# Layer 0's layernorm taken into the loop over heads, its row factors made before the dense sums, and layer 1's constants loaded in layer 0

## The chip, the cores and the metric

The kernel runs on one core of a Trainium2 chip. The metric is the device time of one execution in microseconds (us). Each version was run several times, always beside runs of the kernel before on the same chip. Every run that is compared here is in the fast state. Single executions scatter more than one would like: the kernel before took 4556 to 4594 us over all its runs. The adjacency product of the last layer alone took between 250 and 269 us from trace to trace. So causes are read from the lengths of stages in the traces, which for the stages in question repeat within 1 us, and the total is used only to check them.

## The reference

Four layers follow each other, each as `x = layernorm(x + layer(x))`, over 4096 nodes of 256 features with a 0/1 adjacency. The first two matter here:

```python
# layer 0: eight heads of 32 columns
feats  = (x @ W.T + b).reshape(n, 8, 32)
logit  = leaky_relu(parent[:, None, :] + child[None, :, :], 0.2)   # n x n x heads
logit  = where(adj != 0, logit, 0.0)
out0   = einsum('ijh,jhc->ihc', softmax(logit, axis=1), feats)
# layer 1
out1   = (diagonal(adj) + adj) @ (x @ weight) + bias
```

## The kernel before

The exponential of a leaky sum factors: for one row the terms with a positive sum are a row factor times a column factor, and the others a second such product. So layer 0 needs, for each head, a sum over the neighbours whose sum is positive (a mask that depends on the head) and sums over all neighbours and all nodes (which do not). The latter are the dense sums. Layer 0 is therefore: a prelude (features, logits), the dense sums, the loop over heads, and a closing.

```python
for half in range(2):                      # four heads each
    for it in range(4):                    # a pass: 1024 rows = 8 blocks
        # SyncE: na = packed adjacency of the pass; gm = factored features of the half
        for hh in range(4):                # a head
            # GpSimd's queue: lpb = this head's row logits for 1024 rows, z = its dense sums
            for g in range(8):             # 512 neighbours
                gt = work.tile([P, K, IT], FP8, name="gt", bufs=4)   # masks
                sg = work.tile([P, K, IT], FP8, name="sg", bufs=3)   # signs
                if g % 8 in (2, 5, 7):     # VectorE: 4 comparisons, 1 "and"
                    ...
                else:                      # ScalarE: 4 signs; VectorE: shift and "and"
                    ...
                # TensorE: 32 matmuls with gt as weights
            # VectorE: epilogue of the head (reduce, 6 operations on row factors, divide)
        nc.gpsimd.dma_start(yd[...], y)    # to DRAM
# closing, after the loop: 16 times
nc.sync.dma_start(xs, xr[:, b:b + 2, :]); nc.scalar.dma_start(y, self.yd[b:b + 2]...)
nc.vector.tensor_add(xs, xs, y)
self.layernorm(work, xs, xs)               # statistics on VectorE, power on GpSimd, normalisation on VectorE
```

Layer 1 then loads its weight, bias and the diagonal of the adjacency, makes the support `x @ weight` for 32 blocks, and multiplies it by the adjacency, whose pieces (`adj_piece`) come on SyncE's queue through five buffers. In each of the 32 blocks GpSimd adds one row to X, VectorE adds the product, and a layernorm follows. The order of instructions on each engine is chosen by a scheduler from a timing model, and memory is handed out by pools: a pool that is opened where a closed one lay waits for the closed one's last users (two such waits below took 9.69 and 15.0 us).

## Time and profile before

| | kernel before |
|---|---|
| time | 4570.63 us, median of 3 runs |
| dense sums, first to last matmul | 73.7 to 632.4 us |
| loop over heads | 647.4 to 1352.5 us |
| layer 1's first transpose | 1412.8 us |
| layer 1's last support matmul | 1468.6 us |
| layer 1's adjacency product from there | 246.2 us |

Read such a table by its seams. TensorE is the busiest engine (93% of the span), so the time in which it stands still between two stages is what a reordering may win. The prediction shows the lines.

### The profile page before, as it was taken

The page shows a single profiled execution, that of the slowest core. Times are in us where ns is not written, and L with a number is a line of the kernel's source. Part 1 is how long each engine was busy: PE and PEld are TensorE (multiplying, and loading weights), DVE is VectorE, ACT ScalarE, POOL GpSimd, SP SyncE. Part 2 cuts the span into 40 slices and gives each one's busy share as a digit, 9 for nine tenths or more (in the row PEclk, how much of TensorE's full clock was granted, in tenths as well). Part 3 has the DMA queues.
Part 4 walks back from the last instruction along what each step waited for, and adds up shares of the span by engine and source line. Part 5 has one row for each costly group of instructions (what it writes and reads, how often), then busy time and mean ns, then how long its engine had stood idle before and what let it go on. Part 6 is the DMA issues. An engine that isn't in the chain of part 4 may idle for free. (4 is left out here: it accounts for less than half of the span.)

```text
span 4576.5 us, 71037 instructions
## 1 busy us (share of the span) xinstructions
PE 4252.9 (93%) x25625; PEld 3414.1 (75%) x25625; DVE 3241.1 (71%) x7512; ACT 2638.7 (58%) x5404; POOL 458.8 (10%) x798
## 2 busy tenths in 40 slices
PE   8889989999985999999999999887899999999898
PEld 6889989999984786677777777665666666666676
DVE  6432249999983225977777777488989999999233
ACT  5443359999961005766666666257677777775100
POOL 1344420000002210000000000001000000000010
PEclk9899999999997999999999999999999999999999
DMA  5889972342323884112222222540122222222697
GB/s 164 295 305 318 313 278 79 113 145 78 107 85 90 288 293 148 39 61 79 80 92 86 79 79 78 193 125 30 39 77 74 78 78 78 78 78 77 215 319 256
DMA packets 314075, 637.08 MB, mean 139 GB/s; under 512 B 42855, under 2 KB 114279, under 8 KB 313703
## 3 DMA queue, kind: packets, MB, share of 16 engines
q1 hardware_dynamic: 193734, 421.22, 28.6%
q0 software_dynamic: 34944, 113.54, 7.0%
q10 hardware_dynamic: 85024, 97.58, 6.3%
q8 instruction: 207, 3.39, 0.3%
q14 instruction: 166, 1.35, 0.1%
HBM read 470.71 MB, written 161.48 MB: 138 GB/s over the span
## 5 line engine op out<-in xcount | busy, mean ns | idle before, releaser
L1174 PE MATMUL ps_a<-X,aT 128*128 128x256 f32 x4096 | 963.8, 387 | 26.9 <-ACT aT L1171 26.7
L1174 PEld LDWEIGHTS ps_a<-X,aT 128*128 128x128 f32 x4096 | 762.6, 191 | 292.3 <-ACT aT L1171 135.7
L275 PE MATMUL acc<-gm,gt 128*128 128x198 bf16 x8192 | 701.4, 248 | 14.3 <-DVE sg L260 10.4
L275 PEld LDWEIGHTS <-gt 128*128 128x128 fp8e4 x8192 | 698.7, 97 | 16.9 <-DVE sg L260 10.5
L267 ACT ACTIVATE sg<-lpb,nlc 128x1024 fp8e4<-128x1024 f32 x640 | 670.9, 1135 | 36.4 <-DVE gt L269 19.3
L427 PE MATMUL pz<-src,ar 128*128 128x264 f32 x4096 | 519.4, 289 | 40.1 <-DVE ar L416 39.5
L427 PEld LDWEIGHTS pz<-src,ar 128*128 128x128 f32 x4096 | 513.4, 192 | 46.2 <-DVE ar L416 44.3
L154 PE MATMUL ps_r<-XD,adj_piece 128*128 128x512 f32 x2048 | 508.5, 400 | 14.5 <-DMA adj_piece<-adjs 14.3
L1171 ACT COPY aT<-ps_tp 128x512 f32<-128x512 f32 x512 | 277.4, 583 | 358.6 <-PE ps_tp L1169 354.4
L909 ACT ACTIVATE ja<-e,nc 128x2048 uint8<-128x2048 f32 x240 | 478.7, 1995 | 0.5 <-issue 0.2
L154 PEld LDWEIGHTS ps_r<-XD,adj_piece 128*128 128x128 f32 x2048 | 382.6, 190 | 113.8 <-DMA adj_piece<-adjs 28.0
L836 PE MATMUL ps_logit<-kT,q 64*128 64x512 f32 x1024 | 462.4, 637 | 4.0 <-ACT e L840 3.8
L855 DVE SCALAR_TENSOR_TENSOR v<-e,c 128x4096 bf16<-128x4096 f32 x100 | 447.2, 4472 | 7.3 <-ACT c L883 6.5
L991 DVE MAX8 cand<-v 128x8 f32<-128x256 f32 x1024 | 360.5, 411 | 2.2
L82 POOL TENSOR_SCALAR ln_var<-ln_mv 128x1 f32<-128x1 f32 (+1 forms) x144 | 52.0, 361 | 2972.0 <-DVE ln_mv L80 2733.4
L1038 DVE SCALAR_TENSOR_TENSOR e<-e,edge 128x512 f32<-128x512 f32 x512 | 347.4, 747 | 1.5
L419 ACT ACTIVATE nb<-a 128x512 uint8<-128x512 f32 x256 | 159.4, 630 | 308.2 <-DMA a<-in_adjt_dram 278.0
L1169 PE MATMUL ps_tp<-ident,e 128*128 128x128 f32 x2048 | 273.3, 275 | 38.7 <-DVE e L1038 25.8
L987 DVE SCALAR_TENSOR_TENSOR v<-e,hi 128x2048 f32<-128x2048 f32 x128 | 300.9, 2351 | 1.7
L1169 PEld LDWEIGHTS ps_tp<-ident,e 128*128 128x128 f32 x2048 | 241.9, 142 | 77.2 <-DVE e L1038 29.3
L840 ACT ACTIVATE e<-ps_logit 128x1024 f32<-128x1024 f32 x256 | 261.2, 1021 | 49.7 <-PE ps_logit L836 28.9
L260 DVE TENSOR_SCALAR sg<-lpb,nlc 128x1024 fp8e4<-128x1024 f32 x384 | 273.5, 750 | 2.1
(298 smaller groups left out, 5085.1 us busy)
## 6 DMA issues: line engine op xcount, KB each, us to landing
adj_piece<-adjs SPq DMA_DIRECT2D x256, 512.0 KB, 6.1
adj_piece<-adjs SPq DMA_DIRECT2D x512, 256.0 KB, 3.5
a<-in_adjt_dram SPq DMA_DIRECT2D x256, 256.0 KB, 4.9
adjs<-ar POOLq DMA_DIRECT2D x256, 256.0 KB, 5.5
na<-nad SPq DMA_DIRECT2D x64, 512.0 KB, 4.4
nad<-nb POOLq DMA_DIRECT2D x128, 128.0 KB, 4.7
lpb<-lpd POOLq DMA_DIRECT2D x32, 512.0 KB, 4.2
xfd<-part ACTq DMA_DIRECT2D x63, 256.0 KB, 2.0
```

The lines of the kernel that those rows point to most:

```text
L154: nc.tensor.matmul(ps, a[:, k, :], rhs(jc).rearrange("p s d -> p (s d)"), start=(jc == 0 and own is None), stop=(jc == self.NB - 1))
L267: nc.scalar.activation(sg[:, k, :], lpb, AF.Sign, scale=-1.0, bias=nlc[:, jc, h:h + 1], saturate=False)
L275: nc.tensor.matmul(acc[:, q, :6 * C1], gt[:, k, q * P:(q + 1) * P], gm[:, jc, hh, :], start=(jc == 0 and q % 2 == 0), stop=(jc == NB - 1 a ...
L427: nc.tensor.matmul(pz[q][:, t, :W], ar[:, q, k, :], src[:, jc, t, s], start=(jc == 0 and s == 0), stop=(jc == NB - 1 and s == 1))
L836: nc.tensor.matmul(pl[:, s, :], q[s * A:(s + 1) * A, :], kT[s * A:(s + 1) * A, c * 512:(c + 1) * 512], start=True, stop=True)
L855: nc.vector.scalar_tensor_tensor(junk, e, c, e, op0=ALU.is_ge, op1=ALU.mult, accum_out=S)
L909: nc.scalar.activation(ja, e[:, s * HALF:(s + 1) * HALF], f, bias=nc1, accum_out=fs[:, i + s:i + s + 1])
L987: nc.vector.scalar_tensor_tensor(v, ec, hi, ec, op0=ALU.is_lt, op1=ALU.mult, accum_out=sb[:, s:s + 1])
L991: nc.vector.max(cand[:, 8 * j:8 * j + 8], v[:, k * 256:(k + 1) * 256])
L1038: nc.vector.scalar_tensor_tensor(ec, ec, edge[:, j:j + 1], ec, op0=ALU.is_ge, op1=ALU.mult)
L1169: nc.tensor.transpose(pt[:, k * P:(k + 1) * P], e[:, jc * P:(jc + 1) * P], self.ident)
L1174: nc.tensor.matmul(pa[:, :D], aT[:, k * P:(k + 1) * P], X[:, jc, :], start=(jc == 0), stop=(jc == NB - 1))
```

## The change

The intent: fill the pauses around the heads' loop. The row factors move ahead of the dense sums, so the seam between dense sums and heads gets shorter and the dense results can be stored already multiplied; the residual and the layernorm of a pass are done when its second half is ready, within the loop; layer 1's weight, bias and diagonal are loaded early. The core of the diff, with cuts:

```diff
     def open_x(self):
-        pool = ...tile_pool(name="x", bufs=1)
+        pool = ...tile_pool(name="x", bufs=1, side="right")
...
-            self.sums0(both, lpd, nad, zd, gmd)
-            (row factors fac from lp, lc: 3 reductions, transpose, maximum, exponentials)
-            nc.sync.dma_start(self.fits, fits)
+            self.sums0(both, nlc, fac, lpd, nad, zd, gmd)   # makes fac and fits before its loop
+            self.open_x()
+            self.load1()                                    # w1, bias1: pool on the right, ScalarE's queue
...
+                    if half:
+                        nc.sync.dma_start(X[:, i0:i0 + Q, :], xr[:, i0:i0 + Q, :])
+                        y0 = work.tile([P, Q, D // 2], F32, name="y0", bufs=1)
+                        nc.sync.dma_start(y0, yd[i0:i0 + Q].rearrange("b p d -> p b d"))
...
-                        (six operations on fac and z)
+                        nc.vector.tensor_mul(red, red, fac[:, 0:2, ...])   # one multiply for both factors
+                        nc.vector.tensor_add(t1, t1, red[:, :, 1, :])
+                        nc.vector.tensor_add(t1, t1, z)
...
+                    for q in range(0, Q, 2):
+                        xs = X[:, i0 + q:i0 + q + 2, :]
+                        nc.vector.tensor_add(xs[:, :, :D // 2], xs[:, :, :D // 2], y0[:, q:q + 2])
+                        nc.vector.tensor_add(xs[:, :, D // 2:], xs[:, :, D // 2:], y[:, q:q + 2])
+                        self.layernorm(work, xs, xs)
...
-    def close0(self): (the closing loop)
...
-            w1 = self.load_w(...); bias = ...; diag = ... (layer 1's loads)
```

## The prediction

> **What bounds the kernel now.** I read the page first (one core, TensorE busy 93% of the 4576.5 us span), then the groups of instructions in layer 0, the busy time by stretches, and last the timeline around the three seams that the change touches. By the starts of the groups, layer 0 runs as: a prelude up to 73.7 us, the dense sums to 632.6, the heads' loop from 647.4 to 1352.7, the closing of layer 0 to 1409.4; layer 1's adjacency product starts at 1476.5. Layers 2 and 3 follow and keep their code. From the groups of the first 2000 us:
>
> ```profile
> L275 PE MATMUL acc<-gm,gt 128*128 128x198 bf16 x8192 | 701.4, 248 | 14.3 <-DVE sg L260 10.4 <-DVE gt L262 2.0 <-DVE gt L269 1.4
> L267 ACT ACTIVATE sg<-lpb,nlc 128x1024 fp8e4<-128x1024 f32 x640 | 670.9, 1135 | 36.4 <-DVE gt L269 19.3 <-DVE gt L262 11.9 <-DMA lpb<-lpd 5.1
> L427 PE MATMUL pz<-src,ar 128*128 128x264 f32 x4096 | 519.4, 289 | 40.1 <-DVE ar L416 39.5 <-ACT total L382 0.5
> ```
>
> TensorE waits only 14.3 us in the whole heads' loop, 10.4 of it before the first matmul, and 40.1 us in the dense sums. The busy time by stretches says how near the other engines are (columns: TensorE, its weight loads, VectorE, ScalarE, GpSimd, then clock, DMA share, GB/s):
>
> ```profile
> 900.00:1000.00 100.00, 100.00 (x1178) 100.00 (x1176) 99.17 (x136) 97.25 (x93) 8.15 (x11) 1.00 0.40 127
> 1100.00:1200.00 100.00, 100.00 (x1178) 100.00 (x1176) 99.18 (x135) 96.27 (x93) 9.60 (x12) 1.00 0.32 94
> ```
>
> 1178 matmuls in 100 us are 0.085 us each, and 256 of them 21.75 us per head. But VectorE is 99% and ScalarE 97% busy: three engines are level, and work added to VectorE here is not free. The seams, from the timeline:
>
> ```profile
> 633.16 0.43 DVE L434 TENSOR_TENSOR zt<-total,pz 128x264 f32<-128x264 f32 x1 [1.33 <-ACT zt L433]
> 638.25 1.15 ACT L267 ACTIVATE sg<-lpb,nlc 128x1024 fp8e4<-128x1024 f32 x1 [5.12 <-DMA lpb<-lpd]
> 641.75 0.34 SPq L239 DMA_DIRECT2D na<-nad  x1
> 647.40 10.72 PE L275 MATMUL acc<-gm,gt 128*128 128x198 bf16 x96 [10.37 <-DVE sg L260]
> ...
> 1352.77 1.81 DVE L280 TENSOR_REDUCE red<-acc 128x528 f32<-128x1584 f32 x1 [5.97 <-PE acc L275]
> 1408.69 0.74 DVE L90 TENSOR_SCALAR X<-X,ln_mv,ln_rstd 128x256 f32<-128x256 f32 x2 [1.13 <-POOL ln_rstd L83]
> 1412.81 1.94 PE L102 MATMUL ps_tp<-ident,X 128*128 128x128 f32 x8 [60.08 <-DVEq L452]
> 1418.54 3.75 PE L639 MATMUL ps_sup<-w,xT 128*128 128x256 f32 x8 [3.06 <-DMA w<-in_w_dram]
> 1429.85 0.18 DVE L632 CAST dg<-diag 128x32 fp32r<-128x32 f32 x1 [16.28 <-DMA diag<-in_adjt_dram]
> 1430.44 3.75 PE L639 MATMUL ps_sup<-w,xT 128*128 128x256 f32 x8 [7.93 <-DVE XD L121]
> ```
>
> TensorE stands still 14.8 us between dense sums and heads (the mask loads behind the row factors start only at 641.75), 60 us for the last head's epilogue, the residual with layernorm and the branch, and again until 1430.44 for layer 1's weight and for the diagonal, behind which VectorE, in order, holds the split of the support.
>
> [...] the closing is a regime of its own, with no matmul for 60 us, but the regime it is moved into has VectorE at 99%. [...] The trace has 430 ns as duration and, by successive starts in a head's epilogue (1336.19, 1336.53, 1336.87), 340 ns as pitch. [...] The diagonal is 4096 elements; its load was issued at 1413.79 and was waited for until 1429.85. [...] The first eight matmuls of layer 1 take 3.75 us, later eights 1.99; that price stays.
>
> **The change part by part.**
>
> *Closing.* Removed from the path: the loop over 16 pairs of blocks between 1360.0 and 1409.4, 49.4 us or 3.1 us a pair, of which VectorE works about 2.4 and otherwise waits for GpSimd's power. Only the last pass's four pairs still follow the last matmul: 4 x 3.1 = 12.4 us. The last head's epilogue shrinks from 5.1 us (1352.77 to 1357.8) to about 4.2 (one multiply of 528 elements, 0.71, and two additions of 0.46 in place of six operations, each waiting for the one before). Then the branch, 3.4 us as now. From last matmul to end of layer 0: 56.7 before, 4.2 + 12.4 = 16.6 after. **-40 us.**
>
> *Layer 1's start.* Weight and diagonal lie ready. The second eight matmuls need only the first eight's split: transposes and copies to about 2.3 us after the branch, matmuls cold 3.75, so about 5.5 us after the branch in place of 17.6. **-12 us.**
>
> *Dense to heads.* The loads of mask and factored rows were behind the transfer of the fits flag; in the changed order the first waits for the last matmul and an adjacency write, so near 634 instead of 641.75. Then the row `lpb` limits, as before at 638.2; four signs at 1.04 and one shift-and-mask of 1.22 let matmuls start near 644 instead of 647.4. The first head took 27.75 us by its starts, 6 over the rule, since mask and factored rows (1.3 MB a group) came at 3.3 us a group; most of that goes too. Layer 1's weight load stands ahead of the signs in ScalarE's queue and takes some back. **-7 us**, and another -1 for small waits in the early heads.
>
> *Heads, VectorE.* The epilogue has three multiplies and adds fewer net: 6 x 0.34 = 2.06 become 0.62 + 2 x 0.34 = 1.30, so a head needs 20.7 in place of 21.5 us (12 comparisons at 0.67, 8 masks at 1.15, the reduction 1.72, the rest), against TensorE's 21.75. In the first half this buys nothing. In the second half each pass of four heads gets 8 additions (0.34), 8 statistics (0.33), 8 aggregations (0.08) and 8 normalisations (0.33), 8.6 us, and in the built order they stand nearly in one piece, so that GpSimd's answers are waited for: with 2.6 us of such waits and 1.1 of dependences, 12.3 us, like the 12.4 of the closing. A pass can spare 4 x 1.05 = 4.2 us: a lack of 8.1. Three passes have this inside the loop. For the first I stepped through the order: six groups of masks are ready, TensorE has work to 16.3 us after the head's start, the next group comes at 17.7 and the one after at 22.8, a stall of 3.7. After that no lead is left, and each of the other two costs near 8. Sum 19, and I take 18 as ScalarE and VectorE may fill some waits. **+18 us.**
>
> *Prelude.* The factors now stand before the dense sums, which share the PSUM banks of their transposes: three reductions, transpose, maximum, matmul and copy delay the first dense matmul from 73.7 to about 77: +3.2. The diagonal's load now meets the first loads, where the transfers are saturated from 4 to 12 us; 3479 of its packets ran in the four microseconds from 1424, so it is some 5 us of transfer time beside others: +0.8. **+4 us.**
>
> *Dense sums.* VectorE gets three more operations per block (32 x 3 x 0.43 = 41 us) but waits 225 us there; ScalarE loses 11.8. From 316 us on TensorE never lacks data and the added work, about 2 us at a pair's seam, fits in the 3.9 us that a piece takes. In the first five pairs, where VectorE and ScalarE hold one another up and TensorE loses 9 us a pair, it may cost up to 2 each. **+3 us.**
>
> Sum: 4570.6 - 40 - 12 - 7 - 1 + 18 + 4 + 3 = 4535.6.
>
> **Rivals.** (a) The layernorm is free in the heads' loop: TensorE is the bound there and VectorE's epilogue got shorter. For it: TensorE's wait is 14.3 us. Against: VectorE's 99%. It would give 4518. (b) VectorE becomes the bound of the whole second half, ScalarE's signs (20.8 us of 21.75 a head, through three buffers) lose their rhythm after every burst, and the stall is 35 us or more: 4553. Against: after a burst each head gains 1 us. (c) The dense sums pay: the longer chain before a result's store, and a GpSimd and ScalarE queue that waits in order, repeats the early stalls; 10 to 15 us more: 4548. For it: those stalls are of just this kind; against: the later pairs have 0 to 0.7 us of stall. (d) The waits at layer 1's start are only exchanged for another, say the adjacency pieces: 4545. Against: five pieces are loaded ahead and the support takes over 35 us.
>
> **Range and chances.** The terms are uncertain by about 8 (heads), 7 (dense), 4 (seam), 4 (layer 1) and 4 (closing), together some 13; a range of 1.6 times that either side: 4514 to 4556. Two per cent would be 91 us, more than all that the removed waits hold together (60 + 14.8 + 17.6); slower by as much would need stalls five times those worked out. So within 2% is nearly sure.
>
> **What would show it.** Right: TensorE's gap before layer 1's transposes about 20 us, not 60; the second eight matmuls of the support 5 to 6 us after the branch; VectorE near 100% after the second half's first pass, with three clusters of TensorE waits on masks, 4, 8 and 8 us, each early in a pass; the first half at 21.75 us a head. Wrong: heads of the second half without stalls (rival a), stalls in every head (b), a dense stage longer than 565 us (c), or any change of over 3 us in layers 2 and 3, whose order of instructions I compared and found the same.

## The result, and the profile after

The changed kernel took 4562.97 us (median of 4 runs) against 4571.07 us for the kernel before in the same rounds; the ratio is 0.9975, with a 95% interval of 0.9956 to 0.9995. Ratios here are the mean time of one kernel's fast runs over that of the other's of the same rounds, so not quite the ratio of the two medians. In a second set with 12 runs the ratio was 0.9968. So the change wins 8 to 15 us where 35 were foreseen; 4535.6 was predicted, and the result lies 7 us above the range (4514 to 4556). That it would stay within 2% came true.

The stages of both profiled runs, from the starts of matmuls (us):

| stage | before | after | difference | foreseen |
|---|---|---|---|---|
| first dense matmul at | 73.7 | 76.4 | +2.7 | +4 |
| dense sums | 558.7 | 552.7 | -6.0 | +3 |
| last dense matmul to first heads' matmul | 15.0 | 18.6 | +3.6 | -3 |
| heads 1 and 2 | 50.5 | 46.9 | -3.6 | -4 |
| heads 3 to 32 | 654.6 | 682.5 | +27.9 | +17 |
| last heads' matmul to layer 1's transposes | 60.3 | 19.4 | -40.9 | -40 |
| from there to the last support matmul | 55.8 | 41.6 | -14.2 | -12 |
| layer 1's adjacency product | 246.2 | 253.8 | +7.6 | 0 |

The table ends with layer 1. From there to the end the two traces took 2861.8 and 2869.0 us, a second trace of the changed kernel 2856.0, and two traces of one other kernel (a_early and c_early2) 2872.9 and 2857.8. So the +7.2 of this pair is scatter, and the prediction's sign "any change of over 3 us in layers 2 and 3" cannot be read from single traces.

The groups of instructions of the changed kernel that answer to the three that the prediction shows (same columns; the lines have other numbers in this kernel):

```profile
L242 PE MATMUL acc<-gm,gt 128*128 128x198 bf16 x8192 | 710.2, 250 | 37.7 <-issue 18.3
...
L234 ACT ACTIVATE sg<-lpb,nlc 128x1024 fp8e4<-128x1024 f32 x640 | 670.5, 1135 | 76.5 <-DVE gt L236 38.3
L450 PE MATMUL pz<-src,ar 128*128 128x264 f32 x4096 | 520.9, 290 | 32.5 <-DVE ar L439 26.0
```

TensorE's wait grew from 14.3 to 37.7 us and ScalarE's from 36.4 to 76.5. Part of this stands ahead of the first matmul, in the seam (10.4 us of TensorE's wait before, 18.3 after). Within the loop TensorE's wait grew from 3.9 to 19.4 us, and nearly all of it ends with a mask (`gt`) that VectorE makes. That is the first place to look. The busy time in the 30 us around the end of the second half's first pass, in the kernel before and then in the changed one (columns as in the prediction's second fence):

```profile
1086.00:1116.00 30.00, 30.00 (x355) 30.00 (x354) 29.77 (x40) 28.64 (x29) 2.72 (x4) 1.00 0.29 92
```

```profile
1086.00:1116.00 30.00, 25.14 (x275) 24.28 (x273) 26.38 (x52) 21.34 (x21) 6.58 (x10) 0.94 0.13 42
```

Where TensorE did 355 matmuls, it now does 275. The timeline of the changed kernel says what happens in it (start, length, engine, line, operation, count, and the idle time before with what ended it):

```profile
1099.80 0.75 DVE L267 TENSOR_TENSOR X<-X,y 128x256 f32<-128x256 f32 x2
...
1102.86 0.73 DVE L91 TENSOR_SCALAR X<-X,ln_mv,ln_rstd 128x256 f32<-128x256 f32 x2 [0.86 <-POOL ln_rstd L84]
...
1106.78 1.19 DVE L236 SCALAR_TENSOR_TENSOR gt<-sg,na 128x1024 uint32<-128x1024 uint32 x1
...
1108.00 4.27 ACT L234 ACTIVATE sg<-lpb,nlc 128x1024 fp8e4<-128x1024 f32 x4 [5.27 <-DVE gt L236]
...
1108.02 4.55 PE L242 MATMUL acc<-gm,gt 128*128 128x198 bf16 x32 [2.88 <-DVE gt L236]
...
1114.54 5.66 PE L242 MATMUL acc<-gm,gt 128*128 128x198 bf16 x45 [1.97 <-DVE gt L229]
```

From 1099.80 to 1106.78 VectorE does nothing but layernorm: a clump, as the layernorm of a whole pass in nearly one piece is called below. ScalarE has filled its three buffers of signs and stands for 5.27 us, TensorE runs out of masks for 2.88 us, and the 32 matmuls after that take 4.55 us instead of 2.72: the array's clock has fallen (0.94 over these 30 us, 1.00 before). The next masks come at 1114.54, after another wait of 1.97 us. Heads 21, 25 and 29, the first of each pass with such a clump, took 29.98, 31.44 and 29.82 us; nearly all others took 21.76.

The seam between dense sums and heads, in the changed kernel:

```profile
629.46 2.28 ACTq L463 DMA_DIRECT2D zd<-zt  x2
630.33 0.33 SPq L202 DMA_DIRECT2D na<-nad  x1
630.80 0.54 POOL L213 DMA_DIRECT2D lpb<-lpd  x1 [7.08 <-DVE deg L459]
...
641.05 0.41 ACTq L110 DMA_DIRECT2D w<-in_w_dram  x1
641.07 0.18 DVE L636 CAST dg<-diag 128x32 fp32r<-128x32 f32 x1 [9.69 <-DMA zd<-zt]
...
642.16 10.50 ACT L234 ACTIVATE sg<-lpb,nlc 128x1024 fp8e4<-128x1024 f32 x10 [20.96 <-DVE sg L227]
```

The loads of masks do start early, at 630.33 instead of 641.75. But layer 1's tiles lie on memory that the last dense results (`zt`) used, so the weight's load and the diagonal's conversion wait until those results are stored, which takes until 641, over 9 us after their issue where such a store took 4.8 us in the median before. That the masks' loads, which now stand beside those stores, slow them is likely; no run changed that alone. The signs stand behind the weight's load in ScalarE's queue.

The start of layer 1, where the kernel before had waits of 60.08, 3.06 and 7.93 us:

```profile
1396.49 1.94 PE L103 MATMUL ps_tp<-ident,X 128*128 128x128 f32 x8 [19.10 <-DVEq L272]
1398.30 3.78 PE L645 MATMUL ps_sup<-w,xT 128*128 128x256 f32 x8
...
1402.09 2.12 PE L645 MATMUL ps_sup<-w,xT 128*128 128x256 f32 x8
```

That part is as foreseen. Its adjacency product is not; first TensorE's timeline there in the kernel before, then in the changed one:

```profile
1476.54 20.15 PE L154 MATMUL ps_adj<-XD,adj_piece 128*128 128x512 f32 x88
1501.81 11.18 PE L154 MATMUL ps_adj<-XD,adj_piece 128*128 128x512 f32 x40 [5.12 <-issue]
```

```profile
1446.02 17.18 PE L155 MATMUL ps_adj<-XD,adj_piece 128*128 128x512 f32 x75
1474.71 14.91 PE L155 MATMUL ps_adj<-XD,adj_piece 128*128 128x512 f32 x56 [11.51 <-DMA adj_piece<-adjs]
```

TensorE waits 11.51 us for a piece. The waits of SyncE's queue in the changed kernel from 1390 to 1480 us (total, times, longest) hold this line:

```profile
SPq L152 <- POOL ln_var L83: 15.0, 1, 15.0
```

A load waited 15 us for GpSimd. In the built order (the one that the scheduler made) it is the 11th: a 256 KB piece that is fetched ahead for layer 2, and layer 1's own pieces, of 512 KB, stand behind it. In the kernel before, five such 256 KB pieces were issued from 1418.3 to 1430.2, while layer 1 still made its support, and held up nothing; here the first was issued at 1469.4. So the order of this queue did change.

### The profile page after: what moved, and what is told of

It is laid out like the page before. It is cut to its first block, busy times and chain, and to the rows that moved or that the text cites. A ratio compares the mean times of both kernels' runs of the same rounds, so it can differ in the third digit from the quotient of the medians.

```text
span 4560.9 us, 70953 instructions
## 1 busy us (share of the span) xinstructions
PE 4263.9 (93%) x25625; PEld 3423.7 (75%) x25625; DVE 3254.6 (71%) x7529; ACT 2630.8 (58%) x5373; POOL 458.0 (10%) x794
## 3 DMA queue, kind: packets, MB, share of 16 engines
q1 hardware_dynamic: 197700, 423.31, 28.3%
## 5 line engine op out<-in xcount | busy, mean ns | idle before, releaser
L1180 PE MATMUL ps_a<-X,aT 128*128 128x256 f32 x4096 | 964.2, 387 | 28.9 <-ACT aT L1177 28.8
L242 PE MATMUL acc<-gm,gt 128*128 128x198 bf16 x8192 | 710.2, 250 | 37.7 <-issue 18.3
L234 ACT ACTIVATE sg<-lpb,nlc 128x1024 fp8e4<-128x1024 f32 x640 | 670.5, 1135 | 76.5 <-DVE gt L236 38.3
L155 PEld LDWEIGHTS ps_r<-XD,adj_piece 128*128 128x128 f32 x2048 | 382.7, 189 | 114.0 <-DMA adj_piece<-adjs 27.9
```

Source lines behind the costliest of these rows:

```text
L155: nc.tensor.matmul(ps, a[:, k, :], rhs(jc).rearrange("p s d -> p (s d)"), start=(jc == 0 and own is None), stop=(jc == self.NB - 1))
L234: nc.scalar.activation(sg[:, k, :], lpb, AF.Sign, scale=-1.0, bias=nlc[:, jc, h:h + 1], saturate=False)
L242: nc.tensor.matmul(acc[:, q, :6 * C1], gt[:, k, q * P:(q + 1) * P], gm[:, jc, hh, :], start=(jc == 0 and q % 2 == 0), stop=(jc == NB - 1 a ...
L1180: nc.tensor.matmul(pa[:, :D], aT[:, k * P:(k + 1) * P], X[:, jc, :], start=(jc == 0), stop=(jc == NB - 1))
```

## The experiments

All results were correct. "Heads stage" is from the first to the last heads' matmul: 705.1 us before, 729.4 and 728.8 in two traces of the changed kernel. The last columns of the table are the stretches that the change was about, all from the profiled runs:

| run | ratio to before | gap + heads 1, 2 | heads stage | to transposes | to last support | adjacency |
|---|---|---|---|---|---|---|
| before | 1 | 65.5 | 705.1 | 60.3 | 55.8 | 246.2 |
| changed (a_again) | 0.9968 | 65.4 | 728.8 | 19.4 | 41.4 | 254.4 |
| a_row | 0.9955 | 65.4 | 729.1 | 19.2 | 41.6 | 249.6 |
| a_late | 0.9971 | 64.2 | 730.5 | 19.2 | 40.4 | 254.5 |
| a_early | 0.9984 | 65.2 | 705.0 | 59.1 | 40.8 | 255.9 |
| c_early2 | 0.9993 | 65.9 | 705.1 | 59.6 | 41.3 | 255.9 |
| b_spread | 0.9937 | 65.0 | 715.4 | 19.2 | 41.6 | 253.8 |
| b_pool | 0.9948 | 65.1 | 719.1 | 19.4 | 40.9 | 253.1 |
| b_fill | 0.9956 | 64.9 | 725.3 | 19.4 | 41.7 | 253.5 |
| b_first | 0.9967 | 62.4 | 732.7 | 19.3 | 40.7 | 254.5 |
| c_close | 0.9971 | 64.9 | 720.1 | 27.6 | 41.3 | 254.1 |
| d_pinned | 1.0006 | 65.1 | 700.5 | 63.3 | 40.8 | 253.9 |
| d_deep | 0.9948 | 69.8 | 713.6 | 19.3 | 41.2 | 253.4 |
| d_spreaddeep | 0.9934 | 69.4 | 703.9 | 19.3 | 40.9 | 253.3 |
| c_best | 0.9871 | 62.1 | 711.8 | 15.0 | 41.5 | 239.2 |
| c_bestdeep | 0.9850 | 63.5 | 700.3 | 14.9 | 40.3 | 243.6 |

### The changed kernel again (a_again)

> The changed kernel once more, to be compared in the same rounds as the next three: 4560 to 4565 us, a ratio to the kernel before of 0.997 to 0.999; the same stages as in its first profile within 2 us each (dense 553, heads 729, last heads matmul to layer 1's transposes 19, from there to the last support matmul 42).

Measured: 4557.93 us (12 runs) against 4573.42, 2 us below the expected time. The heads stage, the closing and layer 1 repeat within 1 us. The dense sums do not: 562.0 us here, where 553 was expected, 552.7 in the first trace. So the table's -6.0 for the dense sums is scatter, and the foreseen +3 can be neither confirmed nor refuted.

### Layer 1's row in other memory (a_row)

```diff
+        self.row_at = pool.tile([P, self.D], F32, name="row1")      # in the pool of constants
...
-            row = pool.tile([P, D], F32, name="row1")               # in layer 1's pool
+            row = self.row_at
```

> Only edit: the row that GpSimd adds to all 32 blocks in layer 1 lies in memory that is never given back. Theory (release): in the changed kernel the queue of adjacency pieces stands behind a prefetch for layer 2 that waits until GpSimd has done all 32 additions, because the prefetch's pool overlays the pool that holds this row. Then the stretch from the last support matmul to the end shrinks by about 7 us (3122.8 to about 3116), TensorE's wait of 11.5 us in layer 1's first blocks falls to 5 or less, and the time is about 4556. Rival (additions): GpSimd's 22 us of additions hold up the layernorms, and with them PSUM, whatever the prefetch does; then less than 2 us changes, 4561 to 4564.

Measured: the adjacency product takes 249.6 us, 4.8 less than in the changed kernel of the same job; TensorE's wait of 11.60 us is replaced by two of 4.77 and 2.67. So the release is the cause of 5 of the 8 us. The rest is put down to the rival, GpSimd's additions, which stand ahead of the layernorms in the kernel before too: there GpSimd did 29 of the 32 in one piece from 1477.84 to 1497.97 before it made the first variance, and TensorE's wait of 5.12 us ended at 1501.81. No run changed the additions alone. The total fell by no more than its scatter, 4554.17 against 4557.93.

### Layer 1's weight loaded late (a_late), and the first row loaded first (b_first)

```diff
+                    if half and not it:
+                        nc.sync.dma_start(self.weight1, self.w1.rearrange("(c p) m -> p c m", p=P))
+                        nc.sync.dma_start(self.bias1, row_broadcast(self.b1, D))
...
-        self.weight1, self.bias1 = self.load_w(pool, self.w1, "w1"), self.load_row(pool, self.b1, "bias1")
# b_first, besides:
+                    if not half and not it:
+                        ahead = work.tile([P, IT], F32, name="lpb")
+                        nc.sync.dma_start(ahead, ...)    # ahead of na and gm on the same queue
```

> Only edit: layer 1's weight and bias are loaded by SyncE in the heads' second half, and the converted diagonal has memory of its own, so nothing in ScalarE's or VectorE's queue waits for the last stores of the dense stage. Theory: the first sign starts near 636 instead of 642, the first heads' matmul comes near 642 instead of 647.8, heads stage and layer 1 as in the changed kernel, so 5 to 6 us less: about 4557. Rival (transfers): the first masks and factored rows, 4 MB issued at once, are what the first head waits for; then the first signs come earlier but the first head is that much longer, and the time falls by less than 2 us.

> As the kernel with layer 1's weight loaded late, and the first head's row is loaded on SyncE's queue ahead of the 4 MB of masks and factored rows, not on GpSimd's queue beside them. Theory (transfers): the row landed 9 us after its issue only because the masks and factored rows were issued half a microsecond earlier; now it lands within 3 us, the first signs start near 4 us after the last dense matmul, and the first heads' matmul comes 10 to 12 us after it instead of 16.0 (18.6 in the changed kernel). Rival (the first masks set it): the first group of masks is late now, the gap stays at 15 or more, or the first head grows from 24.6 to 28 us.

Measured for a_late: 16.0 us from the last dense matmul (634.80) to the first heads' matmul, 2.6 less than in the changed kernel where 5 to 6 were expected, and nothing in the total. Its timeline shows what took over:

```profile
635.96 0.33 SPq L203 DMA_DIRECT2D na<-nad  x1
...
636.43 0.54 POOL L217 DMA_DIRECT2D lpb<-lpd  x1 [7.09 <-DVE deg L463]
...
645.21 20.89 ACT L238 ACTIVATE sg<-lpb,nlc 128x1024 fp8e4<-128x1024 f32 x20 [18.30 <-DMA lpb<-lpd]
```

The row `lpb`, 512 KB, was issued half a microsecond after the first masks and was there only 8.7 us later. With the row first on the same queue (b_first, last dense matmul at 638.32):

```profile
639.49 0.33 SPq L205 DMA_DIRECT2D lpb<-lpd  x1
639.87 0.43 SPq L207 DMA_DIRECT2D na<-nad  x1
...
644.58 8.42 ACT L244 ACTIVATE sg<-lpb,nlc 128x1024 fp8e4<-128x1024 f32 x8 [12.74 <-DMA lpb<-lpd]
```

It is there after 5.1 us, and the gap is 11.9 us, as the theory had it. But the first head grows from 24.6 to 28.6 us, as the rival had it: it then waits for masks and factored rows. Both were right, and the sum of gap and first two heads tells what that is worth: 65.4, 64.2, 62.4 us (the changed kernel, a_late, b_first). The total shows nothing of these 3 us: 0.9967 of before. A bound stands behind it: 8 groups of 512 and 792 KB, 10.7 MB with 1 KB as 1024 bytes, take 27 us at the 400 GB/s that the traces show in this stretch (an estimate from these sizes; 406 to 421 GB/s in b_first's slices of 4 us from 652 to 672 us).

So a load on GpSimd's queue, issued 0.47 us after the loads of masks and factored rows began on SyncE's, needed 8.7 us (a_late), and 5.1 us when issued just ahead of them on SyncE's (b_first), where the loads of such a row have a median of 4.1 in both kernels. How the transfers of the two queues share their time was not shown.

### Only layer 1's loads early (a_early, c_early2)

The kernel before with `w1`, `bias1` and `diag` loaded ahead of the dense sums, and nothing else:

```diff
+        right = self.ctx1.enter_context(self.tc.tile_pool(name="l1r", bufs=1, side="right"))
...
+            nc.scalar.dma_start(self.w1_at, ...); nc.scalar.dma_start(self.bias_at, ...)
+            (the diagonal's load)
             pre.close()                     # ahead of the dense sums
```

> The kernel before with one part of the change: weight, bias and diagonal of layer 1 loaded ahead of the dense sums, into memory that nothing else has touched. Theory: the time from layer 1's first transpose to the second eight support matmuls falls from 17.6 to about 5.6 us and to the last support matmul from 55.8 to about 42, while the dense sums, the heads and the closing stay within 2 us of before: 12 to 14 us less than before, about 4558, which would be more than the whole change gave. Rival (exchange): the waits are only taken over by the adjacency pieces or by VectorE's splits; then 2 to 6 us less, 4565 to 4569.

> The kernel before with only layer 1's loads early, once more, because its layer 1 had a median of 0.232 us from matmul to matmul where all other runs had 0.227. If that belongs to this kernel (where its buffers lie), 0.232 comes again and layer 1's adjacency is 254 to 257 us again; if it was that run, 0.227 and about 249.

Measured: the start of layer 1 is 15.0 us shorter (40.8 for 55.8), as the theory had it, and the total only 0.1 to 0.2% lower (ratios 0.9984 and 0.9993). The adjacency product takes 10 us more. About half of that is a steadily slower matmul, which came again in the second run. The busy time of the same stretch in the kernel before, then in c_early2:

```profile
1560.00:1640.00 80.00, 80.00 (x355) 66.26 (x354) 20.53 (x55) 0.00 (x0) 8.56 (x22) 1.00 0.90 306
```

```profile
1560.00:1640.00 80.00, 80.00 (x346) 64.84 (x345) 19.12 (x52) 0.00 (x0) 8.36 (x22) 1.00 0.88 299
```

TensorE is busy throughout, at full clock, and does 346 matmuls for 355: a median of 0.232 us each instead of 0.227. The matmuls are the same; their buffers lie at other addresses. In every run layers 2 and 3 have 0.232 for matmuls of this form; layer 1 has 0.227 in all kernels but this one. Whether the addresses are the cause was not tested. It belongs to the kernel, not to the run, and it means that this experiment cannot price the early loads alone.

### The clumps spread (b_spread)

```diff
+                            if due and g == 3:
+                                now = join(2 * hh, *due)        # additions, statistics, power: one pair
+                            if due and g == 6:
+                                normal(*now)                    # normalisation
```

Each operation is held behind what stands before it on its engine. A first build without that was not run: the scheduler had put the pairs back into one clump.

> Only edit: the residual and layernorm of a pass are held in place in the program, one pair of blocks in each head of the next pass, additions and statistics after the fourth group of masks, normalisation after the seventh; same operations on the same engines. Theory (VectorE's work decides): the 0.9 us waits for GpSimd's power, 3.6 us a pass, are now covered by comparisons, but 4 x 20.7 + 8.6 = 91.4 us of work a pass against TensorE's 87.0 remain, so about 4.4 us for each of three passes: the heads stage falls from 729 to 714 to 719 us, no head over 24.5 us, no matmul slowed after a pause. Rival (the burst is what costs): without one piece of 10 us on VectorE the buffers of masks bridge everything: 705 to 708. Rival (all of it is work): 726 to 730, only spread over more heads.

Measured: heads stage 715.4 us, no head over 24.4, no stall over 1.9 us, no matmuls slowed after one (clock 1.00 from 1180 to 1340 us, 0.96 in the changed kernel). That is the theory's number, in part by luck. The heads of the last two passes took 23.0 to 24.3 us each, so VectorE's work still exceeds TensorE's. But with the 20.5 us a head that is worked out below, 4 x 20.5 + 8.6 = 90.6 us leave 3.6 us a pass, 10.7 for three; the passes lost 2.0, 6.1 and 7.2, 15.3 together. The other 4 to 5 us are no work of VectorE's, and deeper buffers gave them back (d_spreaddeep).

### Additions and normalisation on GpSimd (b_pool)

```diff
-                nc.vector.tensor_add(xs..., y...)      (and the normalisation)
+                nc.gpsimd.tensor_add(xs..., y...)      (and the normalisation)
```

> As the spread kernel, but the residual's additions and the normalisation run on GpSimd, which was 7 per cent busy here; VectorE keeps the statistics. Theory (VectorE's work decides): 4 x 20.7 + 8 x 0.41 = 86.1 us a pass against TensorE's 87.0, so no lack is left: the heads stage 704 to 709 us, each head of passes 2 to 4 of the second half within 0.7 us of 21.76, and the whole 20 to 26 us below the changed kernel. Rival (ScalarE lost its rhythm, not VectorE): over 10 us of stalls remain, 716 or more. Rival (GpSimd in the way of VectorE): the comparisons take longer than 0.67 us wherever GpSimd works, and all heads of the second half lengthen.

Measured: heads stage 719.1 us, worse than with the same work on VectorE. The number alone would fit the second rival too (716 or more); the length of the comparisons decides for the third. The comparisons on VectorE from 1160 to 1360 us, in b_spread and then in b_pool (busy us, mean ns):

```profile
L240 DVE TENSOR_SCALAR sg<-lpb,nlc 128x1024 fp8e4<-128x1024 f32 x106 | 74.3, 747 | 0.5
```

```profile
L240 DVE TENSOR_SCALAR sg<-lpb,nlc 128x1024 fp8e4<-128x1024 f32 x103 | 84.6, 859 | 0.6
```

One comparison takes 859 ns for 747, which on 103 of them is 11.5 us. The masks (1.27 us for 1.21, 42 of them) lose another 2.5. The 33 additions and normalisations that VectorE was spared take about 0.33 us each by successive starts, 10.9 in all. Of the 102 comparisons that began in this stretch, the 36 that overlap no work of GpSimd's took 746 ns on average, as in b_spread, and the 66 others 920, up to 1420. GpSimd's two small operations of a layernorm took 1.84 and 1.37 us within the loop, and 0.22 to 0.30 and 0.71 after it. Its normalisation of 256 columns took 2.52 us on average where VectorE takes 0.41. So in this trace both engines took longer where both worked, and moving work from a full VectorE to GpSimd, which these operations kept busy for 87.1 of the 200 us, lengthened the stage by 3.7 us (719.1 for 715.4). What slows them was not shown.

### TensorE kept busy in the pauses (b_fill)

```diff
+                            if half and it and hh == 0 and g in (6, 7):
+                                for _ in range(60 if g == 6 else 30):
+                                    nc.tensor.matmul(acc[:, 0, 6 * C1:], gm[:, 0, 0, :P], gm[:, 1, 0, :256 - 6 * C1],
+                                                     start=False, stop=False)
```

> Only edit: in the heads after a pass's end (the 21st, 25th and 29th) TensorE gets 60 small matmuls ahead of the seventh and 30 ahead of the eighth group, into columns of the accumulator that nobody reads; the result stays right. They run while the masks are missing and keep the array busy. Theory (masks decide): the 32 matmuls after the pause take 2.7 us again, not 4.6 to 6.5, but TensorE then only waits that much longer for the eighth group's masks; only the slow matmuls after the last pause were on the path, so the heads stage falls by 2 to 4 us, from 729 to about 726. Rival (the clock was the missing term of the bursts): it falls by 8 to 9 us, to about 720.5. If the slowness does not come from the pause, the 32 matmuls stay at over 4 us.

Measured: heads stage 725.3 us, 3.5 to 4.1 less than in the changed kernel: the theory. So the slow matmuls are real but mostly lie where TensorE would have waited for the next masks anyway.

### Layernorm behind the loop (c_close, d_pinned)

```diff
+            for b in range(0, NB, 2):
+                ...
+                nc.vector.tensor_add(xs, xs, yb)        # d_pinned: held behind all of VectorE's earlier work
+                self.layernorm(work, xs, xs)
```

> The changed kernel with one part undone: residual and layernorm stand behind the heads' loop again (X is loaded within it), all else of the change stays. Theory (the three clumps on VectorE make the whole growth of the heads): the heads stage falls from 729 to 700 to 704 us with no head of the second half over 22 us, the stretch from the last heads' matmul to layer 1's transposes is 55 to 60 us again, and the kernel is 12 to 15 us slower than the changed one; the dense sums stay at 550 to 565 and layer 1's start at 42 us. Rival (the new epilogue, the factors or the other order of loads lengthen the heads too): the heads stage stays above 708.

> The kernel that moves the closing behind the loop, now with its additions held behind all of the loop's work on VectorE. Heads stage 700 to 703 with no head of the second half over 22 us, last heads' matmul to layer 1's transposes 55 to 60 us, and 8 to 14 us slower than the changed kernel. If the heads still stay above 708, the changed epilogue itself lengthens them.

Measured for c_close: heads stage 720.1 us and 27.6 us of closing. The expectation failed because the edit did not do what it said: the loads and the layernorms of finished passes were ready, and the scheduler pulled them into the loop again, into heads 23, 24, 27, 28, 31 and 32. Held back (d_pinned), the heads stage is 700.5 us with no head of the second half over 21.9, and TensorE's pause before layer 1 is the old one and 3 us more (55 to 60 were expected):

```profile
1418.31 1.94 PE L103 MATMUL ps_tp<-ident,X 128*128 128x128 f32 x8 [63.09 <-DVEq L268]
```

This is all of the change but its main part, and it is worth nothing in the total: 1.0006. The main part is then worth, by stages, 28.3 us more in the heads (728.8 less 700.5) and 43.9 less in the closing (63.3 less 19.4), so 15.6; the totals of d_pinned and a_again, 1.0006 and 0.9968 of before, say 17, more than the 8 to 14 expected.

The closing kernel (c_close) also shows TensorE's clock after equal pauses, two of 2.07 us. The granted clock of a trace changes only at the borders of steps of 3.41 us (its stretches are multiples of that). For the first pause these are the step in which it lies and the next one; for the second, the step with its larger part and the next one, counted on from the first pause (the clock is the third number from the end):

```profile
1169.92:1173.33 3.41, 1.34 (x17) 1.11 (x15) 3.41 (x4) 0.59 (x2) 0.00 (x0) 1.00 0.25 102
1173.33:1176.74 3.41, 3.41 (x24) 3.11 (x22) 3.41 (x6) 3.41 (x4) 0.46 (x1) 0.50 0.71 181
1241.59:1245.00 3.41, 1.93 (x23) 1.93 (x24) 3.41 (x5) 1.95 (x2) 0.00 (x0) 1.00 0.00 0
1245.00:1248.42 3.42, 3.42 (x43) 3.42 (x41) 3.42 (x8) 3.42 (x5) 0.96 (x1) 1.00 0.11 16
```

The first pause lies whole within one step, which stands idle for 2.07 us, and the next step runs at half clock, with 24 matmuls instead of 43. The second falls across a border, with 0.6 us in one step and 1.48 in the next, and costs no clock. The same count over the heads' loops of all 17 traces (from 20 us after the first matmul) gives 3410 steps at full clock. The 28 that a step at half clock followed stood idle for 1.94 to 3.41 us, the others for at most 1.94. So here it was the idle time within one step, and not the length of the pause, that told whether the clock fell.

### Deeper buffers (d_deep, d_spreaddeep)

```diff
-                            gt = work.tile([P, K, IT], FP8, name="gt", bufs=4)
-                            sg = work.tile([P, K, IT], FP8, name="sg", bufs=3)
+                            gt = work.tile([P, K, IT], FP8, name="gt", bufs=6)
+                            sg = work.tile([P, K, IT], FP8, name="sg", bufs=4)
```

> The changed kernel with six buffers of masks in place of four and four of signs in place of three, nothing else. If VectorE's work decides as the prediction had it (8 us too much a pass), the lead covers 5 us once and the heads stage is 718 to 724 us. If VectorE's need a head is really near 19.9 us (98.3 per cent busy without a stall in the combined kernel with deep buffers, less 6.1 us of layernorm a pass), a clump of 12.3 us meets 7.4 us of spare time a pass and two more groups of lead: stalls of about 9 us in all, heads stage 708 to 714. If only the rhythm of the buffers decides: 700 to 703.

> The spread kernel with the same deeper buffers: all of the layernorm's 8.6 us a pass on VectorE, no waits for GpSimd. With the prediction's 20.7 us a head, 4.4 us a pass are missing and the heads stage is 706 to 711. With 19.9 us a head (4 x 19.9 + 8.6 = 88.2 against 87.0), 1.1 us a pass is missing and the lead covers it: 700 to 704.

Measured: d_deep 713.6, d_spreaddeep 703.9 us, both in the range written for 19.9 us a head. Yet the single heads say that the figure behind these ranges is wrong. In d_deep the second half's later passes take 87.05 + 1.1, + 7.0 and + 6.7 us. In d_spreaddeep no head is long until the 30th (24.88 us); then two follow with 22.64 and 22.68 us. Times four that is 90.6 us a pass, and 90.6 less 8.6 of layernorm leaves 20.5 us a head. Adding up the spacing of VectorE's operations in these traces gives the same: 12 comparisons at 0.66, 8 masks at 1.135, 1.72 + 0.62 + 2 x 0.34 + 0.11 + 0.34 for the epilogue, 20.5 us. With it a clumped pass needs 4 x 20.5 + 8.6 + 3.6 of waits = 94.2, 7.1 more than TensorE's 87.05, as d_deep shows. So the buffers do not remove work. They carry a lead of the first half over to the second, 6 to 7 us by these sums (d_deep lost 14.8 of the 21.4 that three passes lack, d_spreaddeep 5.0 of 10.7). That they also keep ScalarE going through a clump was the author's estimate and was not measured in these two traces.

The larger buffers also lie over other memory: in d_deep the first row's load was issued 9 us after the first masks' instead of 0.5, the gap before the heads grew to 24 us in both kernels, and some 4 us went there.

### The combined kernel (c_best, c_bestdeep)

Layernorm spread; the first half's heads added to X, and half of the statistics taken, within the first half; the first row first, the weight late; layer 1's row in other memory, and GpSimd's additions through three buffers:

```diff
-                nc.gpsimd.tensor_add(xb[:, 0], xb[:, 0], row)            # into X: all 32 can run ahead
+                xb = work.tile([P, 1, D], F32, name="xb", bufs=3)
+                nc.gpsimd.tensor_add(xb[:, 0], X[:, b, :], row)
```

> What the runs point to, together: layernorm one pair in each head of the next pass on VectorE; the first half's heads added to X and half of the statistics taken within the first half, where VectorE has 1 us a head to spare, so the round trip of that half through DRAM goes; weight loaded late and the first head's row first; layer 1's row in memory that is not given back, and its additions on GpSimd into three small buffers, so they cannot run 32 ahead of the layernorms. By the sums: VectorE 4 x 20.7 + 8.6 - 1.4 - 1.1 = 88.8 us a pass against 87.0, heads stage 707 to 712; dense to second head's end 62 to 63 us against 65.5; last matmul to transposes 15 to 17 against 19.3; layer 1's stalls 8 us less. Together 28 to 36 us below the changed kernel, 4524 to 4532 where that has 4558 to 4560. Rival (what is freed is taken back by transfers in layer 3 and the early heads): less than 20.

> As the combined kernel, with six buffers of masks in place of four and four of signs in place of three. Theory (VectorE's sum of work a pass decides): deeper buffers only carry over what VectorE has gained before the first clump, at most 5 us once, so the heads stage is 0 to 5 us shorter than in the combined kernel. Rival (the rhythm of buffers decides): no stall is left and the heads stage is 701 to 703.

Measured: 4519.44 us for c_best (4 runs, 0.9871 of before, interval 0.9841 to 0.9900) and 4509.30 for c_bestdeep (4 runs, 0.9850, interval 0.9821 to 0.9878). Both beat both kernels; c_bestdeep is 1.5% faster than before, and c_best came out below the 4524 to 4532 that were expected. In layer 1 of c_best the waits are nearly gone:

```profile
1417.07 13.54 PE L157 MATMUL ps_adj<-XD,adj_piece 128*128 128x512 f32 x59
1430.89 217.86 PE L157 MATMUL ps_adj<-XD,adj_piece 128*128 128x512 f32 x960 [0.28 <-DMA adj_piece<-adjs]
```

Its product takes 239.2 us, 15 less than in the changed kernel, where 8 were expected. Less the 5 that a_row explains, 10 are left, most likely the additions; but this kernel changes many things at once. (c_bestdeep waits 2.04 us for a piece there again, and takes 243.6.) The heads stage of c_best is 711.8, of c_bestdeep 700.3, the same as without any layernorm in the loop. The expectation of at most 5 us from the buffers failed; the rival's number (701 to 703, no stall left) came true. The buffers gave 11.5 us, of which 3.9 are the first head (28.8 and 24.9 us, after a gap that is 5.3 us longer), so 7.6. VectorE needs 4 x 20.5 + 6.5 = 88.5 us a pass here, 1.4 too many, so over three passes some 4 us that a deeper lead can cover entirely; in c_best, with the shallow buffers, the heads took 22.5 to 23.0 us in the last two passes, 3.5 us a pass above TensorE's time, more than the work alone. The stretch of c_bestdeep that answers to the two of before and after:

```profile
1086.00:1116.00 30.00, 30.00 (x355) 30.00 (x354) 28.73 (x43) 29.18 (x29) 2.40 (x4) 1.00 0.07 24
```

## Why the prediction was wrong

**Closing and layer 1's start** were right: -40.9 for -40, -14.2 for -12. Layer 1's second eight support matmuls began 5.6 us after the first transpose.

**Prelude** +2.7 for +4, right in kind. From 4 to 12 us, where the prediction has the transfers saturated, the DMA share of the kernel before is 1.01 and then 0.87. **Dense sums**: +3 was foreseen, -6 is in the first pair of traces, but the stage scatters from 552 to 570 us over all versions with the new factors, and from 553 to 561 over the three traces without them; this stays open.

**Dense to heads** (-7, of which the step "most of that goes too" for the first head): failed. The loads did start early, but gap and first two heads together took 65.5 us before and after. Three waits in a row hold this seam, and the change removed only the first. Behind it stood the weight's load on reused memory (a_late: 2.6 us of gap), then the row delayed by the masks' loads (b_first: another 4), then the transfer of masks and factored rows itself, which moves the wait into the first head. The prediction saw the weight's load and the transfers, but counted a start made earlier as time won.

**Heads** (+18): right in mechanism, with three clumps where they were foreseen, and mis-sized: +27.9 over heads 3 to 32. The passes lost 8.6, 9.8 and 9.0 us (their four heads' sums less 87.05), 27.4 together; the prediction's 3.7, 8 and 8 make 19.7, which it wrote as 19 and took as 18. Its lead was there: in head 21, which began at 1088.66, six groups of masks were ready and TensorE had work to 16.3 us after that, as stepped. The step that failed comes next: "the next group comes at 17.7 and the one after at 22.8, a stall of 3.7". TensorE got them at 19.4 and 25.9. Without a wait the last would have begun at 19.0, so late masks cost 6.8 us in this pass. Heads 25 and 29 began with the same lead, got these two groups at 20.6 and 27.1, and so lost 8.0 us each to late masks, as foreseen. The other failed term is one that the prediction left out, the cold clock after the pauses: the last group of these three heads took 4.1, 4.4 and 2.7 us instead of 2.72, some 3 us together, near the 3.5 to 4.1 that b_fill gave back. The last 1.5 us lie in other heads. Why the masks of the first clump came 1.6 and 3.1 us later than stepped was not taken apart; VectorE's waits for GpSimd in it, 3.6 us, were in sum as foreseen (2.6, and 1.1 of dependences). A clump also stops ScalarE, for 5.3 us in the first, which with 20.8 of 21.75 us a head has no time to win back. With six and four buffers (d_deep) the passes lost 1.1, 7.0 and 6.7: the sum of work was nearly right (7.1 us by the measured spacings, 8.1 foreseen), but with the buffers of the kernel as it is, each pass lost more than that.

**Layers 1 to 3** (0): failed. "Whose order of instructions I compared and found the same" was not true: the traces show the 256 KB prefetches at the 6th to 10th place of SyncE's queue before, and from the 11th on after. The comparison, which is not on record, went by source lines of the layers, and the loads of adjacency pieces bear the line of a shared helper. X and layer 1's pool moved to the right side of memory, layer 2's buffers came to overlap that pool, and a prefetch for layer 2 had to wait for GpSimd's last addition, in front of layer 1's own pieces: +7.6 us, of which a_row gives back 4.8.

**The sum.** By stages: -40.9 - 14.2 + 2.7 + 0.0 (gap with first heads) + 27.9 + 7.6 = -16.9, without the scattering dense sums; with the foreseen +3 for them, -14. The rounds gave -8 and -15. The three failed terms, 7 for the seam, 11 for the heads (late masks and the cold clock) and 8 for layer 1, less the 4 by which closing, start and prelude came out better, are the distance from the -35 of the prediction. Of the rivals, (a), a free layernorm, is refuted by the heads' +27.9; (c), dense sums that pay, is not settled, for the reason given above; (b), stalls of 35 us or more because ScalarE loses its rhythm, came nearest for the heads, where 27.4 us were lost, but the part of ScalarE's rhythm in them was not taken apart; (d), a wait exchanged at layer 1, was right about adjacency pieces, for a reason that it didn't name.

## What to carry to other kernels

Work that is moved off a pause into a loop where three engines are level costs what it takes there (here 27.9 us over heads 3 to 32): count it against the slack of a period, spread it over the period, and give the producers' buffers room for the largest clump (six and four buffers gave 15.2 us here, 728.8 less 713.6). Keep the pauses that remain short: in the heads' loops of these traces each of the 28 steps of 3.41 us that a step at half clock followed had stood idle for 1.94 us or more, and no step idle for 2 us or more kept the clock after it. A load moved earlier is won only if nothing that the next stage needs first stands beside it or behind it: here loads that began near 630 instead of 641.75 us left the gap with the first two heads at 65.5 us. And where pools and a scheduler decide, compare the order of every engine and queue, helpers included, and look for buffers that come to lie on memory whose last user is late: here a row of 1 KB on the wrong side cost 5 us in the next layer.
